# Exchanging two pairings of small matmuls in a four-layer convolution stack

## The chip, the cores and the metric

The kernel runs on one core of one Trainium2 chip. The metric is the device time of one execution in microseconds (us), and lower is better. Matrix products run on TensorE (PE), other arithmetic on VectorE (DVE), ScalarE (ACT) and GpSimd (POOL). SyncE (SP), ACT and POOL also issue DMA transfers. Every number is float32.

## The reference, cut to what matters

The input is four images of 48 channels and 256 x 256 pixels. Four layers follow one another, each a residual step on the group-normalised image:

```python
x = x + _L0_conv_ref(_gn(x), ...)
x = x + _L1_conv_ref(_gn(x), ...)
x = x + _L2_conv_ref(_gn(x), ...)
x = x + _L3_conv_ref(_gn(x), ...)
```

Layer 0 makes 288 channels with a 1x1 convolution and a 3x3 depthwise one, forms a circular convolution of two thirds of them in 8x8 patches, and gates the last third with it:

```python
hidden = _conv2d(x, w_hidden, b_hidden)
qkv = _conv2d(hidden, w_dw, b_dw, groups=C6, padding='SAME')
q, k, v = jnp.split(qkv, 3, axis=1)
...
out = jnp.fft.irfft2(q_fft * k_fft, s=(PATCH, PATCH))
...
return _conv2d(v * normed, w_out, b_out)
```

Layers 1 and 2 have one form. A 1x1 convolution makes 288 channels, a mask is applied in the frequency domain of 8x8 patches, and a 3x3 depthwise convolution, a gelu gate and another 1x1 convolution follow:

```python
y = jnp.einsum('oc,bchw->bohw', w_in, x)
f = jnp.fft.rfft2(yp) * fft_mask[None]
yp = jnp.fft.irfft2(f, s=(P, P))
...
y = lax.conv_general_dilated(y, w_dw, ..., feature_group_count=C2)
x1, x2 = jnp.split(y, 2, axis=1)
g = jax.nn.gelu(x1, approximate=False) * x2
return jnp.einsum('oc,bchw->bohw', w_out, g)
```

Layer 3 pools, convolves and multiplies; the change doesn't reach it.

## The kernel before, in words

The program is one sequence of stages: `layer0`, then `mix` and `gate` for layer 1, `mix` and `gate` for layer 2, where the second `gate` also runs layer 3 image by image. A tile framework sets the semaphores and chooses the order of the instructions on each engine, from the order in which the program gives them and from the buffers that each tile may turn through (`bufs`).

**Layer 0** works on bands of 8 image rows, 32 bands for each of four images. `conv_step` merges the 1x1 and the depthwise convolution into one contraction over 9 x 48 shifted channels and 10 rows for the biases. It holds 128 of the rows in `k1`, where the three horizontal shifts are three offsets into the same tile, which makes 3 x 128 rows. The other 58 are in `k2`: 48 from three shifts of 16 channels, loaded by three DMAs on SP (L243), and 10 rows of ones, zero at the image's border (L229). A half row of the image is 128 pixels. For each of a band's 16 half rows, one PSUM tile takes three matmuls with `k1` (L252) and then one with `k2` (L256). ACT copies 192 of the 288 columns out (L259), DVE the other 96 (L260). Then `attend_step` for the band before (L274, L292) and `out_step` for the one before that (L331, L344) follow. PSUM is eight tiles of one bank each, all under the tag `ps`.

**Mix** works on 32 steps of each layer, eight for each image, with four patch rows in a step. It first builds `m`, 288 matrices of 64 x 64 that apply the mask, with 128 matmul records of 40 rows (L396). In a step, the *y stage* applies the 1x1 convolution: the 48 normalised channels stand on partitions 0 to 47 for two of the patch rows (`i` = 0) and on 64 to 111 for the other two (`i` = 1), and `w_in` stands on both. The two matmuls of L430 that follow each other take different halves of the partitions and write different PSUM tiles. `evacuate` copies tiles out in turn by ACT (L185) and DVE (L187). DVE also normalises the input (L417). The *z stage* then multiplies each of the 288 channels by its matrix of `m`, two matmuls of 64 x 64 on opposite quarters of the array (L448). Every 16 channels, a PSUM tile of two banks is copied into an output buffer `zo` (four buffers), whose two border columns POOL has cleared (L442, L443). POOL issues two stores for it (L459). The y and z stages share one PSUM pool of four tiles of two banks.

**Gate** reads z back with its borders, applies the depthwise convolution as a matmul (L532), gates (L538, L540), transposes (L556) and projects (L572).

`gn_scalars` computes the mean and the reciprocal deviation of each group for 112 partitions, so that both partition halves have them. Each float32 matmul of the program is two MATMUL and two LDWEIGHTS records in the profile.

## Time and profile before

| | before |
|---|---|
| median of three runs | 22896.4 us (22876.4 to 22939.22) |
| profiled execution, its own time | 22896.4 us |
| its span | 22894.6 us |
| mean granted TensorE clock | 0.845 |
| layer 0 | to 7875 us |
| mix of layer 1, steps only | 7950.9 to 10083.9 us |
| mix of layer 2, steps only | 14688.0 to 16817.7 us |
| PE busy, share of the span | 79% |
| DVE, ACT, POOL busy | 42%, 19%, 20% |

A line of a group of instructions names the line of the kernel, the engine, the operation, what is written and read, the shape and the number. After the bar come the busy time and the mean duration of one in ns, and after the next bar the idle time of the engine ahead of them with what ended it. PE's matmuls overlap, so the mean duration of a matmul is longer than the distance from one to the next. A line of windows gives a stretch's length, then each engine's busy time with the number of its instructions. The clock that was granted to TensorE stands behind them as a share of full speed, followed by the mean DMA share and GB/s. A line of the timeline has a start, a duration and a number of merged instructions.

### The profile page before, as it was taken

How to read it: one execution, taken by the hardware profiler on the slowest of the kernel's cores; microseconds unless marked ns; L12 is line 12 of the kernel's file. 1: busy time of each engine (PE TensorE's matmuls, PEld its weight loads, DVE VectorE, ACT ScalarE, POOL GpSimd, SP SyncE). 2: the span in 40 equal slices, each digit the busy share in tenths (PEclk: the TensorE clock that was granted, in tenths of full speed). 3: DMA queues.
4: the chain of work that ended last, by engine and by line, in shares of the span. 5: the costliest groups of instructions: out<-in, count | busy, mean ns of one | idle time of the engine just before them, and what ended most of it. 6: DMA issues, size and time to landing. Idle time of an engine off the chain costs nothing. (4 is left out here: it accounts for less than half of the span.)

```text
span 22894.6 us, 441693 instructions
## 1 busy us (share of the span) xinstructions
PE 18112.0 (79%) x193104; PEld 11943.0 (52%) x193104; DVE 9680.0 (42%) x13533; ACT 4366.4 (19%) x7626; POOL 4588.6 (20%) x6435
## 2 busy tenths in 40 slices
PE   5998999999999888877777777788877567476473
PEld 3555555555555577765454444577754334244342
DVE  5434433333333444433333333344434554544545
ACT  1111112111111232321111111232221111111110
POOL 0222222222222233320000000133321221311313
PEclk9999999999999899987777777799977667666676
DMA  4222211122122266656666666566656556555554
GB/s 86 45 36 48 41 34 34 34 34 36 32 36 36 42 174 179 176 149 141 138 141 133 133 133 139 130 179 176 172 135 125 109 123 125 113 120 115 122 124 99
DMA packets 744204, 2390.32 MB, mean 104 GB/s; under 512 B 121259, under 2 KB 367553, under 8 KB 681225
## 3 DMA queue, kind: packets, MB, share of 16 engines
q1 hardware_dynamic: 498912, 1414.07, 31.7%
q0 software_dynamic: 217088, 843.24, 13.2%
q10 hardware_dynamic: 26280, 104.75, 2.1%
q8 instruction: 1527, 25.02, 0.5%
q14 instruction: 397, 3.24, 0.1%
HBM read 1381.14 MB, written 845.56 MB: 97 GB/s over the span
## 5 line engine op out<-in xcount | busy, mean ns | idle before, releaser
L532 PE MATMUL c_ps<-ze,d 100*64 100x64 f32 x73728 | 3096.8, 261 | 2384.9 <-DMA ze<-z 1086.9
L532 PEld LDWEIGHTS c_ps<-ze,d 100*64 100x64 f32 x73728 | 3023.7, 174 | 2574.4 <-issue 2302.6
L252 PE MATMUL qkv_ps<-l_wd,k 128*128 128x288 f32 x12288 | 3533.0, 424 | 42.4 <-DMA k<-k 42.4
L572 PE MATMUL xo_ps<-gt,w_out 72*48 72x512 f32 x4096 | 2637.5, 791 | 528.4 <-DVE bm L587 401.3
L252 PEld LDWEIGHTS qkv_ps<-l_wd,k 128*128 128x128 f32 x12288 | 2173.4, 190 | 1309.1 <-issue 850.5
L448 PE MATMUL z_ps<-y,m 64*64 64x64 f32 x73728 | 2290.9, 221 | 444.5 <-issue 377.9
L448 PEld LDWEIGHTS z_ps<-y,m 64*64 64x64 f32 x73728 | 2234.6, 137 | 520.5 <-issue 428.7
L540 DVE TENSOR_TENSOR g<-gl,c_ps 128x512 f32<-128x512 f32 x1152 | 778.7, 685 | 3046.3 <-PE c_ps L532 3034.3
L581 POOL DMA_DIRECT2D x<-xb x256 | 135.4, 529 | 8013.2 <-DVE xb L577 6405.6
L459 POOL DMA_DIRECT2D z<-zo x2304 | 1350.6, 593 | 1561.8 <-ACT zo L185 1010.5
L556 PEld LDWEIGHTS gt_ps<-ident,g 128*72 128x72 f32 x8192 | 1063.9, 168 | 968.9 <-issue 721.4
L260 DVE COPY v<-qkv_ps 128x96 f32<-128x96 f32 x2048 | 495.4, 252 | 2499.9 <-ACT qk L259 2499.8
L256 PE MATMUL qkv_ps<-l_wd,k 58*128 58x288 f32 x4096 | 1529.8, 454 | 0.0
L572 PEld LDWEIGHTS xo_ps<-gt,w_out 72*48 72x48 f32 x4096 | 548.0, 151 | 1862.2 <-issue 1717.1
L430 PE MATMUL y_ps<-w_in,xn 48*128 48x288 f32 x8192 | 1338.3, 461 | 204.9 <-DVE y L187 131.5
L556 PE MATMUL gt_ps<-ident,g 128*72 128x128 f32 x8192 | 1358.8, 326 | 178.7 <-DVE g L540 163.7
L538 ACT ACTIVATE gl<-c_ps 128x512 f32<-128x512 f32 x1152 | 679.4, 595 | 4227.8 <-PE c_ps L532 3553.7
L259 ACT COPY qk<-qkv_ps 128x192 f32<-128x192 f32 x2048 | 648.5, 318 | 4339.2 <-PE qkv_ps L256 4101.4
L187 DVE COPY zo<-z_ps 128x1024 f32<-128x1024 f32 x576 | 704.8, 1224 | 1726.0 <-PE z_ps L448 953.0
L577 DVE TENSOR_TENSOR xb<-xo_ps,xb 48x512 f32<-48x512 f32 x1024 | 698.8, 682 | 1620.3 <-PE xo_ps L572 1616.7
L430 PEld LDWEIGHTS y_ps<-w_in,xn 48*128 48x128 f32 x8192 | 872.4, 205 | 648.5 <-DVE y L187 265.4
L185 ACT COPY gt<-gt_ps 72x512 f32<-72x512 f32 x1024 | 599.5, 585 | 2586.0 <-PE gt_ps L556 2275.8
(107 smaller groups left out, 17952.6 us busy)
## 6 DMA issues: line engine op xcount, KB each, us to landing
z<-zo POOLq DMA_DIRECT2D x2304, 272.0 KB, 5.0
ze<-z SPq DMA_DIRECT2D x768, 815.0 KB
ze<-z SPq DMA_DIRECT2D x3072, 101.9 KB
xa<-x SPq DMA_DIRECT2D x512, 192.0 KB
xb<-x SPq DMA_DIRECT2D x256, 384.0 KB
x<-xb POOLq DMA_DIRECT2D x256, 384.0 KB, 4.9
x<-in_x SPq DMA_DIRECT2D x120, 480.0 KB
k<-k SPq DMA_DIRECT2D x128, 387.0 KB
```

Source lines behind the costliest of these rows:

```text
L187: nc.vector.tensor_copy(dst, src)
L252: nc.tensor.matmul(ps[:, :C6], k1[:, r, w0 + k : w0 + k + 128], w1[:, k, :], start=(k == 0), stop=False,)
L256: nc.tensor.matmul(ps[:, :C6], k2[:, r, w0 : w0 + 128], w2, start=False, stop=True)
L430: nc.tensor.matmul(ps[i][:, n, :C6], xn[at, j + n].rearrange("p u r c -> p (u r c)"), w_in[at], start=True, stop=True,)
L448: nc.tensor.matmul(ps[u : u + 64, k // 8, 64 * (k % 8) : 64 * (k % 8) + 64], m[u : u + 64, c, :], y[u : u + 64, c, :], start=True, stop=True,)
L459: nc.gpsimd.dma_start(zs[b][:, row : row + 2, 16 * g : 16 * g + 16, :], z[64 * u : 64 * u + 64],)
L532: nc.tensor.matmul(ps[u][p0 : p0 + 64, f0 : f0 + 64], d[:, HID * u + 48 * n + cc, :], ze[u][:, :, cc, 0:NP], start=True, stop=True,)
L538: nc.scalar.activation(gl, ps[0], AF.Gelu)
L540: nc.vector.tensor_tensor(g[:, q0 : q0 + 8, :], gl.rearrange("p (q j) -> p q j", q=8), ps[1].rearrange("p (q j) -> p q j", q=8), ALU.mult,)
L556: nc.tensor.transpose(ps[:72, 128 * q : 128 * q + 128], g[:, :, 32 * i + j + v + q], ident,)
L572: nc.tensor.matmul(ps[:C, :], w_out[:, u, :], gt[:, :, u, :], start=(u == 0), stop=(u == 1),)
L577: nc.vector.tensor_tensor(xv, ps[:C, :].rearrange("p (j r c) -> p r j c", r=P, c=P), xv, ALU.add)
```

## The change

In layer 0, the 58 leftover rows are put on both halves of the partitions. `k2` has 122 partitions and half the rows: image rows 0 to 3 of a band stand on partitions 0 to 57, rows 4 to 7 on 64 to 121. The weights `w2` stand on both. The conv loop takes four half rows at a time, two from each half, with four PSUM tiles open. Their four `k2` matmuls go first, alternating halves, and then three `k1` matmuls follow for each tile with its two copies. The `k2` loads are six per band, each of half the size, and the loads of ones are two.

In the mixes, the channels stand on 48 partitions only. The matmuls of the y stage are done for one `i` after the other, on one partition half, with a PSUM pool of its own (two tiles of two banks). The z stage groups 24 channels per output buffer, with three buffers instead of four. A PSUM tile is one bank of eight channels (four tiles), so an output buffer takes three copies of 512 columns. There are 24 stores per step instead of 36. The group means are computed for 48 partitions.

```diff
-            wh2, w2 = weight("l0_wh2", [58, C6]), weight("l0_wd2", [58, C6])
+            wh2 = wp.tile([122, C6], F32, tag="l0_wh2", name="l0_wh2")
+            w2 = wp.tile([122, C6], F32, tag="l0_wd2", name="l0_wd2")
+            for p0 in (0, 64):
+                nc.scalar.dma_start(wh2[p0 : p0 + 58], t["l0_wh2"])
+                nc.scalar.dma_start(w2[p0 : p0 + 58], t["l0_wd2"])
...
-                k2 = sb.tile([58, P, W], F32, tag="k2", name=f"k2_{key}")
+                k2 = sb.tile([122, P // 2, W], F32, tag="k2", name=f"k2_{key}")
...
-                nc.sync.dma_start(k2[48:58], t["ones"][kind])
+                for i in range(2):
+                    nc.sync.dma_start(
+                        k2[64 * i + 48 : 64 * i + 58], t["ones"][kind, :, 4 * i : 4 * i + 4]
+                    )
...
                 for k in range(3):
-                    nc.sync.dma_start(
-                        k2[16 * k : 16 * k + 16], k1[32:48, 2 : P + 2, k : k + W]
-                    )
+                    for i in range(2):
+                        nc.sync.dma_start(
+                            k2[64 * i + 16 * k : 64 * i + 16 * k + 16],
+                            k1[32:48, 2 + 4 * i : 6 + 4 * i, k : k + W],
+                        )
...
-                for g in range(2 * P):
-                    r, w0 = g // 2, 128 * (g % 2)
-                    ps = psum.tile([128, 512], F32, tag="ps", name=f"qkv_ps_{key}_{g}")
-                    for k in range(3):
+                for r in range(P // 2):
+                    gs = [(i, h) for h in range(2) for i in range(2)]
+                    ps = {
+                        (i, h): psum.tile([128, 512], F32, tag="ps", name=f"qkv_ps_{key}_{r}_{i}_{h}")
+                        for i, h in gs
+                    }
+                    for i, h in gs:
+                        at = slice(64 * i, 64 * i + 58)
                         nc.tensor.matmul(
-                            ps[:, :C6], k1[:, r, w0 + k : w0 + k + 128], w1[:, k, :],
-                            start=(k == 0), stop=False,
+                            ps[i, h][:, :C6], k2[at, r, 128 * h : 128 * h + 128], w2[at],
+                            start=True, stop=False,
                         )
-                    nc.tensor.matmul(
-                        ps[:, :C6], k2[:, r, w0 : w0 + 128], w2, start=False, stop=True
-                    )
-                    nc.scalar.copy(qk[:, g, :], ps[:, : 2 * C2])
-                    nc.vector.tensor_copy(v[:, g, :], ps[:, 2 * C2 : C6])
+                    for i, h in gs:
+                        row, w0 = r + 4 * i, 128 * h
+                        for k in range(3):
+                            nc.tensor.matmul(
+                                ps[i, h][:, :C6], k1[:, row, w0 + k : w0 + k + 128], w1[:, k, :],
+                                start=False, stop=(k == 2),
+                            )
+                        g = 2 * row + h
+                        nc.scalar.copy(qk[:, g, :], ps[i, h][:, : 2 * C2])
+                        nc.vector.tensor_copy(v[:, g, :], ps[i, h][:, 2 * C2 : C6])
...
+            psum2 = st.enter_context(tc.tile_pool(name=f"a{layer}ps2", bufs=2, space=PSUM))
...
-                        for j in range(0, 16, 2):
-                            ps = [
-                                psum.tile([128, 2, 512], F32, tag="ps2", name=f"y_ps_{key}_{h}_{j}_{i}")
-                                for i in range(2)
-                            ]
-                            for n in range(2):
-                                for i in range(2):
-                                    at = slice(64 * i, 64 * i + C)
+                            for j in range(0, 16, 2):
+                                ps = psum2.tile([128, 2, 512], F32, tag="ps2", name=f"y_ps_{key}_{i}_{h}_{j}")
+                                for n in range(2):
                                     nc.tensor.matmul(
-                                        ps[i][:, n, :C6],
-                                        xn[at, j + n].rearrange("p u r c -> p (u r c)"),
-                                        w_in[at], start=True, stop=True,
+                                        ps[:, n, :C6], xn[:, j + n].rearrange("p u r c -> p (u r c)"),
+                                        w_in, start=True, stop=True,
                                     )
...
-                    for g in range(C6 // 16):
-                        z = sb.tile([128, 2, 16, CW], F32, tag="zo", name=f"zo_{key}_{g}", bufs=4)
+                    for g in range(C6 // 24):
+                        z = sb.tile([128, 2, 24, CW], F32, tag="zo", name=f"zo_{key}_{g}", bufs=3)
...
-                        ps = psum.tile([128, 2, 512], F32, tag="ps2", name=f"z_ps_{key}_{g}")
-                        for k in range(16):
-                            c = 16 * g + k
+                        for n in range(3):
+                            ps = psum.tile([128, 512], F32, tag="ps", name=f"z_ps_{key}_{g}_{n}")
+                            for k in range(8):
+                                c = 24 * g + 8 * n + k
...
```

## The prediction

> **What bounds the kernel now.** I read the busy slices first. They show three regimes: TensorE (PE) at 9 tenths with the full clock up to slice 14 (layer 0), dense work with much DMA in the two mix passes, and a lower clock in the gates. The change touches layer 0 and the mixes only, so I cut the span at the first and last instruction of each: layer 0 runs to 7875 us, the mixes take 7950.90 to 10083.90 and 14688.00 to 16817.70.

> ```profile
> PE   5998999999999888877777777788877567476473
> PEclk9999999999999899987777777799977667666676
> L252 PE MATMUL qkv_ps<-l_wd,k 128*128 128x288 f32 x12288 | 3533.0, 424 | 42.4 <-DMA k<-k 42.4
> L256 PE MATMUL qkv_ps<-l_wd,k 58*128 58x288 f32 x4096 | 1529.8, 454 | 0.0
> ```

> PE waits only 42.4 us for the conv inputs of layer 0. It is the bound there. Each float32 matmul is two MATMUL records. The timeline of PE gives their pace:

> ```profile
> 5002.06 1.72 PE L252 MATMUL qkv_ps<-l_wd,k 128*128 128x288 f32 x6
> 5003.71 0.75 PE L256 MATMUL qkv_ps<-l_wd,k 58*128 58x288 f32 x2
> 5004.39 1.72 PE L252 MATMUL qkv_ps<-l_wd,k 128*128 128x288 f32 x6
> ```

> One half row takes 5004.39 - 5002.06 = 2.33 us for eight records. By their start times, records of one shape follow each other after 0.2425 us, but the last record before a change of shape takes 0.33 and the first after it 0.35. So each switch between 128 and 58 rows costs 0.19 us.

> In the mixes I read the windows of single y stages (L430) and of the z stage (L448) that follows:

> ```profile
> 8355.17:8378.24 23.07, 19.03 (x131) 12.32 (x129) 16.17 (x22) 10.38 (x16) 3.70 (x14) 1.00 0.53 122
> 8378.24:8421.73 43.49, 36.45 (x1153) 35.56 (x1153) 12.76 (x12) 9.40 (x9) 21.57 (x58) 0.96 0.75 209
> 16557.56:16587.11 29.55, 26.12 (x131) 17.27 (x129) 17.41 (x23) 11.44 (x17) 7.21 (x24) 0.71 0.52 122
> 7884.00:7944.00 60.00, 60.00 (x126) 41.62 (x125) 19.84 (x31) 19.86 (x31) 0.00 (x0) 0.50 0.04 11
> ```

> After length and PE, PEld, DVE, ACT and POOL busy come the granted clock, DMA share and GB/s. A y stage takes 23.1 us, but 29.6 where the clock is 0.71. Over 64 steps y averages 24.8 us and z 41.8. The last line, building m, matters most: 40-row matmuls run back to back, PE is 60.00 of 60.00 us busy, and the clock never leaves 0.50. Each record takes 0.48 us.

> [...] in the timeline, eight 48-row records, alternating halves, take four slots of 0.2425 us:

> ```profile
> 8363.12 1.24 PE L430 MATMUL y_ps<-w_in,xn 48*128 48x288 f32 x8 [0.17 <-ACT y L185]
> ```

> [...] the m stage is all busy and stays at half. So I summed, per 3.413 us window, rows/128 x streaming time at full clock (L532's two column halves share their rows, so half of each counts). Of windows under 0.33, and over 0.05, 3 of 1000 were followed by full clock; over 0.38, 4440 of 4443. Between 0.33 and 0.355 it was 16 of 167. The limit is near 0.36, for rising and falling alike. It predicts the m stage: 40/128 x 0.5 = 0.16. The slow y stage above shows it too: its windows at half clock have 0.31, 0.35, 0.34, 0.36, and after one of 0.375 the clock is back.

> ```profile
> 16568.72:16572.14 3.42, 3.42 (x16) 0.50 0.41 92
> 16572.14:16575.55 3.41, 3.41 (x16) 0.50 0.31 84
> 16575.55:16578.96 3.41, 2.51 (x20) 1.00 0.00 0
> ```

> **The change, part by part.**

> *Layer 0.* Before, four half rows take 4 x 2.33 = 9.32 us. After, the four 58-row matmuls come first, alternating halves like the y pairs: eight records in four slots. From the first of them to the first 128-row record: 0.01 + 0.35 + 3 x 0.24 + the pair offsets + 0.33 = 1.19 us, or 2.13 if the halves don't overlap. Then 24 records of 128 rows: 0.35 + 22 x 0.2425 + 0.33 = 6.02. Together 7.21, so 2.11 us less per block. There are 4 images x 32 bands x 4 = 512 blocks: **-1081 us**, or -600 (8.15 us a block) without overlap. PE stays the bound: a band goes from 58.1 to 49.7 us, while per band DVE is busy 3165/128 = 24.7, POOL 13.3 and ACT 11.5. PSUM: four tiles open at once of eight; a block's tiles are copied out (0.32 ACT, 0.25 DVE each) one by one while the next block runs 7.2 us. On SP, three k2 loads (median 1.84 us to issue) become six of half the size, and one ones load (0.29) becomes two: +0.3 to +3 us per band. They are queued behind the k1 copies and ahead of the next band's loads on SP, and a matmul that waits for k2 holds all of PE's queue. The chain from normalising (5004.7) to the last k2 load landed, about 5016, ends 18 us before the next conv at 5034.5; losing 8 us of conv still leaves 10. Only at each image's first band is it exposed (the 42.4 us were these four); k2 now comes first on PE but last on SP: +25 us, bounds 0 and 50. I take 20 us for waits in attend and out that the shorter conv covers less. Sum: **-1036**, bounds -1090 and -580.

> *y stage.* Pairs become single 48-row matmuls: 128 records x 0.2425 = 31.0 us at full clock, not 15.5. A tile takes 0.97 us and two buffers turn. DVE starts 0.43 us after the last record's start, copies for 0.76, and PE resumes 0.06 later: 0.73 + 0.43 + 0.76 + 0.06 = 1.98 against 1.94, plus 0.1 for a weight load no longer hidden. So two tiles take 2.08. The occupancy is then 48/128 x 0.99 x 1.94/2.08 = **0.346**, under 0.36 even before the eight 0.81 us normalisings on DVE stall it further. The clock drops, and at half clock 48 rows give 0.19: it can't rise before z. I take the rest of the window in which y starts (1.7 us) and 1.3 windows more at full clock, with one step in five cold from the start: 4.9 us for 4.7 tiles, then 27.3 x 1.92 = 52.4. So y takes **57 us**, bounds 35 (no drop: 32 x 1.04 and 2 for normalising) and 61.4 (all cold: 128 x 0.48).

> *z stage.* The matmuls stay: 288 channels x 0.117 = 33.7 us of PE; the rest of 41.8 is waiting for output buffers:

> ```profile
> L459 POOL DMA_DIRECT2D z<-zo x2304 | 1350.6, 593 | 1561.8 <-ACT zo L185 1010.5 <-DVE zo L187 318.7 <-issue 116.8
> L442 POOL MEMSET zo<- 128x32 f32 x1152 | 203.9, 181 | 1238.3 <-DMA z<-zo 1104.1 <-PE m_ps L396 133.5
> ```

> Groups of 24 in three buffers hold 72 channels, not 64; POOL issues 24 stores per step instead of 36 (-7 us of 28 on POOL, at 0.59 each); a store carries half as much again, at the same rate. Against it, PSUM holds 32 channels ahead of the copies rather than 64, so PE leaves z about 32 channels later (2.4 us per 16: +4.9), and z starts at half clock for a window (+1.7). The wait of a memset for a store holds the stores queued behind it on POOL, whose new order I can't see. I take 43, bounds 37 (DMA rate) and 48.

> *The rest* (loading w_in once, group means on 48 partitions, 512-column copies: 36 x 0.63 us on two engines under 34 us of PE) hides beside PE; if not, it costs a few us in all.

> Mixes: 64 x (57 + 43 - 66.6) = **+2138 us**. Total: the profiled execution lasted 22896.4 (span 22894.6, 1.8 around it) and is itself the median of the runs. 22896 - 1036 + 2138 = **24,000 us**.

> **The rivals.**

> *Faster: the clock holds in y.* If PE stalls less than 0.11 us per 3.4 us window (occupancy 0.36 instead of 0.346), 48 rows keep the full clock, y takes 35 and z 42: 64 x (35 + 42 - 66.6) = +666, giving 22,530 us. For it: full-speed 48 rows without stalls give 0.371, just above the limit. Against it: two tiles per 2.085 us is what y shows now after a DVE-limited pair, with four buffers to turn instead of two.

> *Half held:* y loses the clock only midway, at about 45 us: 64 x 21.4 = +1370, giving 23,230. For it: of 17 full-clock windows between 0.34 and 0.36, 6 were followed by full clock. Against: one low window ends it.

> *Layer 0's pairs don't overlap:* -555 in place of -1036, giving 24,480. Against: the y pairs, the same pattern, do.

> *z at PE's pace:* y cold, z at 37: 23,610, inside the range.

> **How the numbers follow.** Clock lost early: 0.82 (with z and both layer-0 variants), clock held: 0.12, half held: 0.06. The forecast's own bounds, y 53 to 61 and z 38 to 47 against -1036, are 23,420 and 24,510. They leave some 0.05 of the first case out, and down to 23,300 half of the half-held case comes in. Range 23,300 to 24,530. This measurement can tell about 0.3% (69 us) from no change. Faster 0.12, same 0.01, slower 0.87.

> **What would show it.** Windows of single y stages: clock near 0.55 and 55 to 61 us if right; 1.00 and 35 if wrong. A timeline of layer 0: x8 L256 then x24 L252, blocks of 7.2 us, layer 0 ending near 6840. z near 43 with POOL's memsets still waiting for stores. I am wrong if y keeps the clock, or if layer 0 stays above 7200.

## The result, and the profile after

| | before | after |
|---|---|---|
| median | 22886.4 us (4 runs, 22810.65 to 22939.22) | 24137.9 us (4 runs, 24093.23 to 24219.9) |
| ratio to before | | 1.0554, 95% interval 1.051 to 1.0597 |
| span of the profiled execution | 22894.6 us | 24091.5 us |
| mean granted TensorE clock | 0.845 | 0.78 |
| first y matmul of layer 1 (layer 0 and m built) | 7950.9 us | 6940.1 us |
| steps of the two mixes | 2133.0 + 2129.7 us | 3230.5 + 3253.5 us |
| y and z stage, mean of 64 steps | 24.8 and 41.8 us | 58.4 and 42.9 us |

The kernel became 5.5% slower. The two spans differ by 1196.9 us: layer 0 gave 1010.8 back, the mixes took 1097.5 + 1123.8 more, and the rest came out 13.6 shorter. The page of the kernel after shows the place. Its clock row falls from 9 to 6 or 7 in slices 12 to 17 and again in slices 25 to 30, where the mixes now lie, and the y matmuls (L444, before L430) have moved up to third place:

```profile
PEclk9999999999977767677777776776777667666676
L444 PE MATMUL y_ps<-w_in,xn 48*128 48x288 f32 x8192 | 3743.8, 653 | 59.2 <-ACT y L182 47.1
L275 PE MATMUL qkv_ps<-l_wd,k 128*128 128x288 f32 x12288 | 3132.2, 412 | 0.0
L472 POOL DMA_DIRECT2D z<-zo x1536 | 902.5, 592 | 4332.8 <-ACT zo L182 3855.0
```

The same 8192 records that lasted 461 ns each now last 653, and PE waits only 59 us for them. So y isn't slower because it waits; it is slower while it works. PE doesn't wait in front of layer 0's 128-row matmuls (L275) at all now. POOL's idle time in the last group is not a new wait on the path: POOL waits for ACT's copies because y takes so long.

The windows of one step, y stage and then z stage, say why. The fields are those of the lines of before: length, busy time of PE, PEld, DVE, ACT and POOL, then the clock:

```profile
7147.40:7203.30 55.90, 55.90 (x126) 38.56 (x126) 17.42 (x24) 9.64 (x15) 2.01 (x8) 0.54 0.22 54
7203.30:7246.20 42.90, 38.78 (x1157) 37.78 (x1156) 12.69 (x20) 11.47 (x19) 15.50 (x40) 0.92 0.73 205
```

```profile
7148.35:7151.76 3.41, 3.41 (x15) 2.33 (x14) 0.79 (x2) 1.29 (x2) 1.45 (x4) 1.00 0.87 279
7151.76:7155.17 3.41, 3.41 (x9) 2.38 (x8) 0.72 (x1) 0.65 (x1) 0.28 (x2) 0.50 0.67 178
```

The occupancy of a window is an estimate of mine: rows/128 x streaming time at full clock, summed over its records and divided by its length. For a record of 288 columns I take 0.24 us, half of its measured pace of 0.48 us at half clock. Of the first window's records, 13.5 streams fall inside it: 13.5 x 0.24 x 48/128 / 3.41 = 0.355. The second and every later one up to z is at half clock with about 0.19.

Layer 0 does what its slots promised. This is its timeline, with start, duration, line and number of records:

```profile
5021.93 1.24 PE L268 MATMUL qkv_ps<-l_wd,k 58*128 58x288 f32 x8
5023.10 6.09 PE L275 MATMUL qkv_ps<-l_wd,k 128*128 128x288 f32 x24
5029.11 1.24 PE L268 MATMUL qkv_ps<-l_wd,k 58*128 58x288 f32 x8
```

A block of four half rows takes 5029.11 - 5021.93 = 7.18 us, and the eight records of 58 rows take 1.17 of it.

### The profile page after: what moved, and what is told of

It is laid out like the page before. It is cut to its first block, busy times and chain, and to the rows that moved or that the text cites. A ratio compares the mean times of both kernels' runs of the same rounds, so it can differ in the third digit from the quotient of the medians.

```text
span 24091.5 us, 443476 instructions
## 1 busy us (share of the span) xinstructions
PE 19549.9 (81%) x193104; PEld 13634.3 (57%) x193104; DVE 9736.0 (40%) x14110; ACT 4444.6 (18%) x8202; POOL 4091.1 (17%) x4899
## 5 line engine op out<-in xcount | busy, mean ns | idle before, releaser
L444 PE MATMUL y_ps<-w_in,xn 48*128 48x288 f32 x8192 | 3743.8, 653 | 59.2 <-ACT y L182 47.1
L444 PEld LDWEIGHTS y_ps<-w_in,xn 48*128 48x128 f32 x8192 | 2556.0, 314 | 1179.4 <-issue 196.4
L275 PE MATMUL qkv_ps<-l_wd,k 128*128 128x288 f32 x12288 | 3132.2, 412 | 0.0
L275 PEld LDWEIGHTS qkv_ps<-l_wd,k 128*128 128x128 f32 x12288 | 2300.5, 191 | 798.3 <-issue 202.9
L461 PEld LDWEIGHTS z_ps<-y,m 64*64 64x64 f32 x73728 | 2349.6, 143 | 412.9 <-issue 352.7
L184 DVE COPY y<-y_ps 128x576 f32<-128x576 f32 x1024 | 775.6, 757 | 2549.9 <-PE y_ps L444 2549.9
L472 POOL DMA_DIRECT2D z<-zo x1536 | 902.5, 592 | 4332.8 <-ACT zo L182 3855.0
L184 DVE COPY zo<-z_ps 128x512 f32<-128x512 f32 x1152 | 793.9, 691 | 2005.8 <-PE z_ps L461 1301.5
L182 ACT COPY y<-y_ps 128x576 f32<-128x576 f32 x1024 | 658.1, 643 | 2892.7 <-PE y_ps L444 2864.5
L182 ACT COPY zo<-z_ps 128x512 f32<-128x512 f32 x1152 | 689.4, 602 | 2256.0 <-PE z_ps L461 1794.4
```

Of the source, the lines that this page charges most:

```text
L182: nc.scalar.copy(dst, src)
L184: nc.vector.tensor_copy(dst, src)
L275: nc.tensor.matmul(ps[i, h][:, :C6], k1[:, row, w0 + k : w0 + k + 128], w1[:, k, :], start=False, stop=(k == 2),)
L444: nc.tensor.matmul(ps[:, n, :C6], xn[:, j + n].rearrange("p u r c -> p (u r c)"), w_in, start=True, stop=True,)
L461: nc.tensor.matmul(ps[u : u + 64, 64 * k : 64 * k + 64], m[u : u + 64, c, :], y[u : u + 64, c, :], start=True, stop=True,)
L472: nc.gpsimd.dma_start(zs[b][:, row : row + 2, 24 * g : 24 * g + 24, :], z[64 * u : 64 * u + 64],)
```

## The experiments

The theory was that the y stage is slow because 48 rows at a time don't hold the clock (0.54 in the stage above), and that layer 0 gains two things, fewer switches of shape and two halves at once. The rivals: y is slow for its lost pairs and its fewer PSUM buffers alone, or the total came out right from two wrong parts. The table has means of the 64 mix steps. Runs e3, e4, e5 and e8 are single ones; as the fifteen runs of before beside e1 to e4 lie between 22806 and 22948 us, differences of 100 us between times are not read without the traces.

| run | time, us | y, us | y stages under 46 us | z, us |
|---|---|---|---|---|
| before | 22886.4 | 24.8 | 64 | 41.8 |
| after | 24137.9 | 58.4 | 0 | 42.9 |
| e1_both: before, layer 0 of after | 21832.82 | 25.9 | 64 | 41.3 |
| e2_rows64: after, 64 rows in y | 22895.83 | 42.0 | 44 | 42.2 |
| e3_rows52: after, 52 rows in y | 24035.15 | 57.4 | 0 | 43.3 |
| e4_psum3: after, three PSUM tiles for y | 24066.49 | 57.1 | 0 | 43.3 |
| e5_one_half: after, layer 0 on one half | 24622.67 | 58.4 | 0 | 43.0 |
| e6_rows128: after, 128 rows in y | 22483.6 | 34.3 | 64 | 42.5 |
| e7_both_128: e1 with 2 x 64 rows in y | 21825.79 | 23.9 | 64 | 42.0 |
| e8_zero16: e2, added rows stream zeros | 23082.29 | 43.1 | 41 | 42.2 |

### e1_both: the layer-0 part alone

The edit is the hunks of `layer0` from the diff, put into the kernel before; `mix` keeps its pairs.

> The kernel before with the changed layer 0 alone, so that the mixes keep their pairs. Theory: layer 0 gives 2.11 us per block of four half rows, 512 blocks, and the whole loss of the change is in the mixes. Then 22,886 - 1,036 = about 21,850 us, layer 0 ends near 6,860 us and the mix steps stay at 66.6 us. Rival: the layer-0 gain is smaller, and the mixes cost less than they seem to (the total came out right by two errors): 22,300 us or more.

It took 21832.82 us, a ratio of 0.9545 to before (0.9504 to 0.9586), with y at 25.9 and z at 41.3 us, 67.2 together. The building of `m` for layer 1 starts at 6868.9 us. So layer 0's pairs are worth 1,038 us against the runs of before beside it (22870.51 us), and the mix part of the change costs the difference to after, 24137.9 - 21832.8 = 2,305 us. The total didn't come out right from two wrong parts. This version beats both kernels.

### e2_rows64 and e3_rows52: the same work with more rows

```diff
-            w_in = wp.tile([C, C6], F32, tag="w_in", name=f"w_in_{layer}")
-            nc.scalar.dma_start(w_in, t[f"l{layer}_w_in"])
+            w_in = wp.tile([RY, C6], F32, tag="w_in", name=f"w_in_{layer}")
+            nc.scalar.dma_start(w_in[:C], t[f"l{layer}_w_in"])
+            nc.scalar.dma_start(w_in[C:], t[f"l{layer}_w_in"][: RY - C])
+            nc.vector.tensor_scalar(w_in, w_in, share, None, ALU.mult)
...
-                                nc.sync.dma_start(xt[:, u], x_of[b][:, r0 : r0 + P, cols])
+                                nc.sync.dma_start(xt[:C, u], x_of[b][:, r0 : r0 + P, cols])
+                                nc.sync.dma_start(xt[C:, u], x_of[b][: RY - C, r0 : r0 + P, cols])
```

`RY` is 64 or 52. `share` is 0.5 for a channel that stands twice and 1 for the others; `xt`, `xn` and the group means have `RY` partitions.

> The changed kernel with 64 rows in each y matmul in place of 48: channels 0 to 15 stand a second time on partitions 48 to 63, and each of the two copies has half the weight. Same number of matmuls, tiles, copies, buffers and stalls. Theory (rows x time sets the clock): occupancy 64/128 x 0.99 x 0.93 = 0.46, over 0.36, so the clock stays full, y takes about 36 us per step in place of 58, z starts at full clock: 22,600 to 22,800 us. Rival (y is slow for its lost pairs and its two PSUM buffers, whatever the rows): no change, 24,140 us, or a little more for a third more input loads.

> The same with 52 rows: channels 0 to 3 twice, half the weight each. Theory: occupancy 52/128 x 0.99 x 0.93 = 0.375 without further stalls, a little over the limit of 0.36; windows with a normalising step between the copies fall below it, and from then on the clock stays half. So y between 40 and 55 us, 23,000 to 24,000 us. [...] If the limit were much lower than 0.36, it would be as with 64 rows.

With 64 rows it took 22895.83 us, 5% less than after, level with before (ratio 0.9992, 0.9964 to 1.002). Apart from the loads of the second copies, nothing but rows was added, and 44 of the 64 y stages fell to 32.3 us. That excludes the rival that lost pairs and fewer buffers alone make y slow; what they cost at full clock is 32.3 - 24.8 = 7.5 us a step. It also excludes that 48 rows count like 64. The run missed the expected 22,600 to 22,800 because the other 20 stages stayed slow. One of each kind, as windows:

```profile
7326.58:7358.91 32.33, 32.33 (x124) 21.85 (x124) 16.15 (x23) 9.78 (x15) 2.33 (x8) 1.00 0.42 106
7402.33:7461.61 59.28, 59.28 (x124) 40.89 (x124) 17.39 (x24) 9.63 (x15) 2.02 (x8) 0.50 0.22 57
```

The same 124 records take 32.33 us at full clock and 59.28 at half. The window in which a stage begins tells the two kinds apart. It still holds the end of z and PE's wait ahead of y. Seven of the slow stages began at half clock. The other 13, the one shown among them, began at full clock and lost it with that window, whose occupancy was 0.21 to 0.37; in the 44 fast stages it was 0.376 or more. Afterwards nothing changes: 64 rows at half clock reach 0.25 at most, and none of this run's 330 windows with y alone at half clock was followed by full clock. The twelve runs spread accordingly, from 22718 us at a mean clock of 0.834 to 23075 at 0.82.

With 52 rows it took 24035.15 us, only 103 less than after, and the miss is instructive. I put the full-clock windows with y alone in order of their occupancy. From 0.38 up, 21 of 22 were followed by full clock; between 0.37 and 0.38, 4 of 11, the four fullest (0.373); between 0.36 and 0.37, 0 of 18. For these matmuls the windows that kept the clock and those that lost it part between 0.37 and 0.38 rather than at 0.36, as they did for the stages of e2. 52 rows reach 0.385 in most of their windows from 0.38 up, and one emptier window ends it: in no stage did the clock hold. The measure is less exact for other shapes. In the y pairs of the kernel before, 5 of 8 full-clock windows between 0.36 and 0.37 held the clock, and over all its matmuls 105 of 300 windows between 0.355 and 0.38 were followed by full clock. (L532's records count half there: on the two column halves, two of them start every 58 ns at full clock.)

### e4_psum3: 48 rows without the stalls

```diff
-            psum2 = st.enter_context(tc.tile_pool(name=f"a{layer}ps2", bufs=2, space=PSUM))
-            psum = st.enter_context(tc.tile_pool(name=f"a{layer}ps", bufs=4, space=PSUM))
+            psum2 = st.enter_context(tc.tile_pool(name=f"a{layer}ps2", bufs=3, space=PSUM))
+            psum = st.enter_context(tc.tile_pool(name=f"a{layer}ps", bufs=2, space=PSUM))
```

> The changed kernel with three PSUM tiles for y in place of two, and two one-bank tiles for z in place of four. 48 rows stay. Theory: without PE's stalls for DVE's copies the occupancy is up to 0.371, just over the limit, so in steps that enter y at full clock it holds for much of the stage: y between 32 and 57 us by step, 40 to 50 on average, 23,100 to 23,700 us, if z doesn't get slower. Rival (rows alone decide, stalls don't matter): y stays at 57 us, 24,140 us.

It took 24066.49 us, with y at 57.1. The third tile does remove the stalls, and the clock falls nevertheless:

```profile
7358.17:7361.58 3.41, 3.41 (x16) 2.63 (x15) 1.05 (x3) 1.29 (x2) 1.26 (x4) 1.00 0.84 224
7361.58:7364.99 3.41, 3.41 (x9) 2.35 (x8) 2.12 (x3) 0.66 (x1) 0.28 (x2) 0.50 0.38 96
```

The first window has a record every 0.2425 us, the pace of records without waits here and in layer 0 alike: 48/128 x 0.24/0.2425 = 0.371. Half clock follows it, and so it did after all 25 full-clock windows of this run at 0.37 with y alone. The expectation was wrong because it took 0.36 for the limit. At this pace 48 rows make no more than 0.371, so by these 25 windows I estimate that no order of these matmuls alone would have held the clock here.

### e6_rows128 and e8_zero16: recovery, and what counts as a row

In e6, `RY` is 128, channels 0 to 31 stand three times and the others twice. In e8, `RY` is 64 and the weights of the added rows are zero (these lines show the change against e2):

```diff
-            nc.scalar.dma_start(w_in[C:], t[f"l{layer}_w_in"][: RY - C])
-            nc.vector.tensor_scalar(w_in, w_in, share, None, ALU.mult)
+            nc.vector.memset(w_in[32:], 0.0)
+            nc.scalar.dma_start(w_in[:C], t[f"l{layer}_w_in"])
```

> The changed kernel with 128 rows in each y matmul: channels 0 to 31 three times, 32 to 47 twice, with weights of a third or a half. Theory: with 64 rows, the steps that entered y at half clock stayed there, because 64 rows at half clock give 0.25. 128 rows at half clock give 0.5, over the limit, so a cold step recovers within one or two windows, and all 64 steps take 32 to 36 us: 64 x (34 + 42 - 101.3) = -1,620, about 22,500 us, though the input loads are 2.7 times as large. Rival (the slow steps have another cause): some 20 steps stay at 57 to 63 us, 22,900 us or more.

> As with 64 rows, but the weights of the 16 added rows are zero, and the first 48 rows have their full weights: 64 rows are switched on, and 16 of them stream zeros. If the clock follows the rows that an instruction switches on: as with 64 rows in use, 22,900 us, most y stages at 32 us. If it follows the data in them: as with 48 rows, 24,140 us, y at 57 us.

With 128 rows it took 22483.6 us, a ratio of 0.9829 to before (0.98 to 0.9858). Nine of its y stages began at half clock and five lost full clock with the window in which they began, 14 in all against 20 in e2. Yet no y stage exceeds 41 us. So the slow stages of e2 were those that had lost the clock and couldn't get it back. One that keeps it here, and one that loses it at first:

```profile
7251.89:7284.30 32.41, 32.41 (x125) 22.18 (x125) 16.18 (x23) 9.85 (x15) 1.73 (x6) 1.00 0.64 129
7635.30:7669.31 34.01, 34.01 (x125) 23.25 (x125) 16.18 (x23) 9.84 (x15) 1.75 (x6) 0.95 0.62 122
```

In e8, 41 of the 64 stages are at about 32.4 us, as against 44 in e2 and none with 48 rows. One of each kind:

```profile
7269.84:7302.19 32.35, 32.35 (x125) 21.85 (x125) 16.16 (x23) 9.74 (x15) 1.73 (x6) 1.00 0.37 90
7344.75:7404.56 59.81, 59.81 (x124) 41.12 (x124) 17.38 (x24) 9.64 (x15) 2.01 (x8) 0.50 0.23 59
```

With 16 of 64 rows at zero weight the stages are thus like those with 64 weighted rows, and not like those with 48: in these runs the clock went with the rows of an instruction, those of zero weight included. Its 23082.29 us are one run. The profiled execution of e2 took 147 us less: 71 of this lie in the mixes, where three more slow stages cost about 3 x 27 = 81 us, and 69 in the gate of layer 1 (up to the first y matmul of layer 2), whose program is the same in both.

### e5_one_half: what the halves add in layer 0

```diff
-                        at = slice(64 * i, 64 * i + 58)
                         nc.tensor.matmul(
-                            ps[i, h][:, :C6], k2[at, r, 128 * h : 128 * h + 128], w2[at],
+                            ps[i, h][:, :C6], k2[:, r + 4 * i, 128 * h : 128 * h + 128], w2,
                             start=True, stop=False,
                         )
```

`k2`, `w2` and their loads are those of before.

> The changed kernel with layer 0's four 58-row matmuls still first, but all on partitions 0 to 57, as before. Theory: the halves run together, so losing that costs 0.94 us per block (eight slots of 0.2425 us in place of four): 512 x 0.94 = +481, 24,620 us, with a block of 8.15 us. Rival: the gain of layer 0 came from fewer switches of shape alone: no change, 24,140 us, and a block of 7.2 us.

It took 24622.67 us, 485 more than after. In its timeline a block takes 5011.48 - 5003.33 = 8.15 us:

```profile
5003.33 2.20 PE L259 MATMUL qkv_ps<-l_wd,k 58*128 58x288 f32 x8
5005.46 6.09 PE L266 MATMUL qkv_ps<-l_wd,k 128*128 128x288 f32 x24
5011.48 2.20 PE L259 MATMUL qkv_ps<-l_wd,k 58*128 58x288 f32 x8
```

On one half the eight records take 2.13 us, on two 1.17. Over 512 blocks the difference of 8.15 and 7.18 is 497 us. In the two profiled executions the first y matmul of layer 1 comes 567 us apart, 70 more. That is again the clock: 37 blocks of e5, of which 36 are the first of their band, are about 3.3 us longer because they run in part at half clock. In after there are five such blocks. The window ahead of the block shown here, with the waits that end the band before and the first of these matmuls, had an occupancy of 0.354. This block of e5 and the one behind it, in windows of PE alone with the clock, DMA share and GB/s:

```profile
2770.90:2782.38 11.48, 11.48 (x33) 0.70 0.40 79
2782.38:2790.53 8.15, 8.15 (x33) 1.00 0.00 0
```

In all, blocks touched by half clock lost 133 us in e5 and 32 in after; PE's idle time in layer 0, 20 us less in e5, goes the other way.

So the gain of layer 0 has both sources. By blocks it is 497 us from the halves running together, and 512 x (9.32 - 8.15) = 599 us from six switches of shape fewer per block (6 x 0.195 = 1.17). By the first y matmul of layer 1, with the waits and the clock, the switches are worth 444 us (7950.9 - 7507.0) and the halves 567.

### e7_both_128: more rows in the kernel with both pairings

Each half of the y pairs is filled up to 64 rows as in e2, in the kernel of e1.

> The kernel with both pairings, each half of the y pairs filled up to 64 rows by channels 0 to 15 a second time, half the weight each. Theory: the y pairs have 96 rows, 0.371 to 0.375 at half clock, so a fifth of their records run at half clock; with 128 rows they recover at once, and y goes from 25.9 to about 23.3 us per step: -170 us, 21,660 us. Rival: the input loads, a third larger, or the copies by ACT and DVE set y's pace: 21,830 us or more.

It took 21825.79 us, a ratio of 0.9533 (0.951 to 0.9555), which can't be told from e1's. The mechanism acted: y went from 25.9 to 23.9 us, and the share of its records at half clock from 21% to 5% (13% in before, where the mixes are those of e1). But z took 0.7 us longer per step, so the mixes gained 64 x 1.3 = 82 us, and of the two spans (21816.5 and 21797.0) only 20 us is left. Of the other 60, 53 lie in the gate of layer 1, which no edit touched: in the ten profiled executions it lasts from 4563 us (e1) to 4666 (e4).

## Why the prediction was right, step by step

**Forecast.** 24,000 us against 24137.9, in the range, and by the forecast's own mechanism. The profiled execution, 24093 us, lies 93 above the forecast: layer 0 gave 25 less than forecast, the mixes took 83 more (2221 in place of 2138), and the rest came out 14 shorter.

**Layer 0's blocks.** 7.21 us forecast, 7.18 measured; 8.15 without overlap forecast, 8.15 measured in e5. The two halves overlap as the y pairs of before did. One sum is written wrongly: four slots have two distances of 0.24 between the first and the last, not three. With two the 1.19 us come out, and 1.17 were measured; with three it would be 1.41.

**Waits added in layer 0.** 45 us were taken (25 for k2 at each image's start, 20 for less cover). The blocks gave 512 x (9.32 - 7.18) = 1,096 and layer 0 ended 1,011 earlier, so 85 were lost. Up to the building of `m`, PE is idle for 665.7 us in place of 598.2, which is 67 of it. The rest is about what blocks lost that half clock touched: 32 us in place of 2, waits inside them included. The list of PE's waits gives the idle time in small pieces, each as total, times and longest. The wait for k2 is 17 us longer than the one for k1 was (42.4):

```profile
PE qkv_ps L268 <- DMA k<-k: 59.6, 5, 17.8
PE f L295 <- DVE v L281: 18.0, 12, 3.4
PE qkv_ps L268 <- DVE v L281: 8.8, 6, 3.2
```

The second and third lines are new. A conv that opens four PSUM tiles at once, and the matmuls after it, now catch up with DVE's copies at a few places. So the term of 45 us was about 40 too small, and its sign was right.

**y stage.** 57 us forecast, 58.4 measured: 57.2 in the stage, and 1.2 for four records that the framework moved into the middle of z. Two tiles at full clock take 2.08 us as forecast. The 0.1 us that it added shows in the trace as the start of a record after a wait: 0.346 us to the next one in place of 0.2425 (at 7147.40). In the stage of 7147.40 the clock falls after the first full window, of 0.355, and the rest runs at 0.48 us a record. The forecast put 4.7 of a stage's 32 tiles ahead of the fall; on average it was 3.9 (12% of the y records run at full clock). It had one stage in five beginning cold, and 4 of 64 did, but 37 more lost the clock with the window in which they began.

**The limit** was mis-sized: 0.36 forecast, between 0.37 and 0.38 measured for single y matmuls. Nor was it alike for rising and falling: of all windows of before between 0.355 and 0.37, 21 of 29 at full clock were followed by full clock, but 14 of 169 at half clock. It didn't hurt the total, since 0.346 is below both. It made the main rival look possible. "If PE stalls less than 0.11 us" can't save 48 rows, which e4 showed.

**z stage.** 43 us forecast, 42.9 measured. Its parts weren't tried one by one. When y leaves at full clock more often z is 42.2 (e2) or 42.5 (e6), so the cold start is worth some 0.4 to 1 us rather than 1.7. As the total is right, another part is off by about as much the other way, and that they cancel is luck. POOL's memsets still wait for stores, as forecast: 581.8 us in the mix of layer 1, against 552.5 before.

**The rivals.** The held clock and the half-held clock are excluded by the windows of y, and layer-0 halves that don't overlap by the timelines of after and e5. z at PE's pace didn't come about.

## What to carry to other kernels

A stage of matmuls with few rows can be slow while PE looks fully busy, as here with 48 rows (55.90 of 55.90 us busy at a clock of 0.54): put the granted clock of that stage beside its busy time before looking for waits. For matmuls like these, estimate the occupancy, rows/128 x streaming time, for each window of 3.41 us at the clock of the moment, for the stage entered at full clock and at half; in these runs the windows of single y matmuls that kept the clock and those that lost it parted between 0.37 and 0.38; another kernel has to be measured anew. Pairing two small matmuls on opposite partition halves paid twice here, in slots and in clock, in the y stage (24.8 us a step against 32.3 for single matmuls of 64 rows at full clock and 58.4 in after) and in layer 0 (497 us by blocks and 70 more in e5) alike, and where no pair was at hand, spreading the contraction over more rows with the weight divided among the copies recovered 1,650 us of the 2,305 lost here, with more arithmetic and more input loads.

## What the runs showed of the hardware that was not expected

- For single y matmuls little separates keeping the clock from losing it: 48 rows without any stall made 0.371 and lost it (25 of 25 windows of e4), while 52 rows kept it in 21 of 22 windows from 0.38 up (e3).
- Rows with zero weights counted for the clock like weighted ones: 41 of 64 stages at full clock (e8), against 44 with weights (e2) and none with 48 rows.
- The y stage of e2 had two durations: the same 124 records of 64 rows took 32.33 or 59.28 us, by the clock that it had after the window in which it began (occupancy 0.37 or less in the 13 stages that lost it, 0.376 or more in the 44 that kept it).
